# Position norms in groups of three chunks, zeroed states by copy, and new timetables

## The chip, the cores and the metric

The kernel runs on one core of a Trainium2 chip. The metric is the device time of one execution in microseconds, as the median of several runs. A profiled execution is one more run, recorded by the hardware profiler; its span is the time from the first to the last recorded instruction.

Five engines work side by side, each in the order of its own instructions: PE (matmuls; PEld are its weight loads), DVE (vector work), ACT (activation functions and copies), POOL (vector work of another kind) and SP, which here only issues DMA transfers.

## The reference, cut to what matters

The input x is 8 images of 256 channels and 48 x 48 positions (N = 2304). The parts that the change touches are these:

```
# layer 0, per image (after a group norm of x), with a residual
pos  = pos / max(norm(pos), 1e-12)
sim  = pos @ pos.T
topksim, topkid = top_k(sim, 16)
out  = sum(softmax(topksim) * feat[topkid])

# layer 1: two mamba layers in a row, with a group norm and a residual
dA = exp(dt_t[:, :, None] * A)
h  = h * dA + dt_t[:, :, None] * B_t[:, None, :] * x_t[:, :, None]
y  = einsum('bds,bs->bd', h, C_t)          # h starts as zeros
```

Each mamba layer has 512 inner channels and 16 states for each of them; A is minus the exponential of A_log. A layer also has a layer norm over the channels, an input projection, a convolution of four taps, a step size dt by softplus, a gate by silu and an output projection.

## The kernel before, in words

**Units.** The positions of an image are cut into six chunks of T = 384. A unit is one chunk c at one of the two mamba depths d. The 12 units of an image are run in the order (c,d) = (0,0), (1,0), (2,0), (0,1), (3,0), (1,1), (4,0), (2,1), (5,0), (3,1), (4,1), (5,1). The text calls these places positions 0 to 11 of an image. Positions 0 and 3 are the units with c = 0, in which the state begins as zeros.

**Steps and hooks.** A unit is 16 steps of 32 inner channels. The 128 partitions of a step are its 32 channels times four groups of states, with four states in each partition; a half takes two of these four. A half is a "hook": 32 hooks make a unit. Each hook has one scan on DVE (`run_scan`, L932, 128 x 770), whose factors are the decays that ACT makes by two exponentials (`decay`, L917) one hook ahead, in two PSUM banks. The scan's other input bx is made by POOL two steps ahead (`make_bx`, L893), and its first column is the state carried over from the chunk before. `take_up` (one step ahead) puts this in: an ACT copy out of `h_st` (L907), or for c = 0 a POOL memset (L905). After the scan the states are multiplied by C: on POOL for the halves with "G" in `SHARE` (`pool_part`, L960, issued a step later; two neighbouring halves in one instruction), on DVE for those with "V" (L934). `SHARE` has a row for each stage, see below. PE sums the states of four steps into y (`sum_states`, L975 and L978), the gate (L984) uses y, and ACT keeps the last column (`carry`, L948; `carry_pool`, L970).

**dt and dtx rows.** A step's rows come back from HBM in a replicated form by `load_rep` (L639), issued on SP: "dt" into one of three fixed buffers (step number modulo three), "dtx" into a pool of three.

**Timetables.** All else that a unit needs (input weights `load_in`, projections `in_proj`, taps, softplus, silu, gates, output projection) stands in two tables, `between` and `behind`, of entries (hook, function, arguments). A hook may be negative, since a unit's preparation lies in earlier units. At each hook the program issues, in this order:

```
        carry(m - 1)
        decay(m + 1)
        if p == 0:
            make_bx(n + LEAD)
            pool_part(n - 1)
            take_up(n + 1)
        else:
            carry_pool(n - 1)
```

then the `between` entries of that hook, the scan, the `behind` entries, and one piece of layer 0 of a later image (`ahead.go`). Nothing is reordered after that: the order of the program is each engine's order. There are three pairs of tables, one for each stage: beside the top-k of a later image (positions 1 to 9), `between_spare` and `behind_spare` (positions 10, 11 and 0), and the last image's own. An entry's stage goes by where its hook in the first pair lies.

**Layer 0 ahead.** `layer0` is a generator; each `yield` ends a hook's piece. Its projections and norms for image b run from hook 11 of position 11 of image b - 2 to about hook 28 of position 0 of image b - 1; its 18 blocks of similarities and top-k, 16 hooks each, then fill positions 1 to 9. Image 0's runs alone at the start. For a chunk, PE makes two projections (pp) and three features (pf), ACT copies them out (pos L363, feat L372) and squares pos, PE sums the norms (pn) and ACT takes them out into n2 (L377). The inverse root is Ln and Exp on ACT (`rsqrt_start`, L167 and L168) and one Newton step of five instructions on POOL (`rsqrt_end`, L175 to L179). `scale` spreads the result rn by PE (pb, L232) and multiplies pos by it on DVE (L324). All of this is done for each chunk, one chunk behind the projections.

Of the kernel before, what the change touches and what calls it, by code (L numbers as in the profile page):

```python
# [9 lines left out]
F32 = mybir.dt.float32  # L10
BF16 = mybir.dt.bfloat16
AF = mybir.ActivationFunctionType
# [4 lines left out]
P = 128  # L17
# [9 lines left out]
def tile_conv_preact(  # L27
# [46 lines left out]


    SHARE = (
        "GGVGGGVGGGVVGGVGGGGVGGGVGGGGGVVG",
        "GVGGGVVVGGVVGGGVVGGGVGVVGGVVGVGV",
        "VVVGVVGGGVVVGGVVGGGVGGVVVVGGGVVG",
    )  # L80
    assert N % T == 0 and N % P == 0 and T % P == 0 and NS % (J * HQ) == 0

# [145 lines left out]
    def spread(cols, n, psum, name):  # L228

        pb = psum(n * P, name)  # L230
        for j in range(n):
            nc.tensor.matmul(  # L232
                pb[:, j * P : (j + 1) * P], cols[:, j : j + 1].to_broadcast([P, P]), ident,
                start=True, stop=True,
            )
        return pb
# [24 lines left out]
    def layer0(b, left, pool, ps0, alone):  # L261
# [7 lines left out]
        def step(make, use):  # L269

            if len(pending) == depth:
                leave_psum()
            pending.append((make(), use))

        def leave_psum():
            if pending:
                made, use = pending.pop(0)
                use(made)
# [18 lines left out]
        pos = pool.tile([P, CB, N], F32, tag="pos", name=f"pos_{b}", bufs=1)  # L297
        feat = pool.tile([P, NB, C], F32, tag="feat", name=f"feat_{b}", bufs=1)
        n2, rn = {}, {}

        def normalized(c):
            xn = loaded.pop(c)
# [7 lines left out]
            return xn  # L310

        def inverse_norm(c):
            rn[c] = small.tile([P, TB], F32, tag="rn", name=f"rn_{b}_{c}")
            rsqrt_start(rn[c], n2[c], tiny[:, 1:2])

        def inverse_norm_end(c):
            rsqrt_end(nc.gpsimd, rn[c], n2[c], TINY, f"rn_{b}_{c}")

        def scale(c):


            def use(pb):
                cs = slice(c * T, (c + 1) * T)
                nc.vector.tensor_tensor(  # L324
                    pos[:, :, cs], pos[:, :, cs], pb.unsqueeze(1).to_broadcast([P, CB, T]), ALU.mult
                )

            step(lambda: spread(rn[c], TB, mm0, f"pb_{b}_{c}"), use)

        def chunk(c, xn):  # L330
            cs = slice(c * T, (c + 1) * T)
# [40 lines left out]
                return lambda pf: nc.scalar.copy(feat[:, c * TB + j, :], pf)  # L372

            def norm(pn):
                n2[c] = small.tile([P, TB], F32, tag="n2", name=f"n2_{b}_{c}")

                nc.scalar.activation(n2[c], pn, AF.Relu, bias=tiny[:, 0:1])  # L377

            for ob in range(CB):
                step(lambda: project(ob), position(ob))  # L380
# [12 lines left out]
        for c in range(NCH):  # L393
            yield from chunk(c, xn)
            if c + 1 < NCH:
                xn = normalized(c + 1)
            yield
            if c > 0:
                scale(c - 1)
                yield  # L400
        while pending:
            leave_psum()
# [3 lines left out]
        inverse_norm_end(NCH - 1)  # L406
        yield
        yield
        scale(NCH - 1)
        yield  # L410
        leave_psum()
        yield

        x1 = hbm.tile([C, N], F32, tag="x1", name=f"x1_{b}")
# [462 lines left out]
    def at(n):  # L877

        return units[n // STEPS], n % STEPS, n % STEPS // J
# [6 lines left out]
    def make_bx(n):  # L886


        if not 0 <= n < NSTEP:
            return  # L890
        unit, i, k = at(n)
        bx = keep.tile([P, Q, 1 + T], F32, tag="bx", name=f"bx_{n}", bufs=8)
        nc.gpsimd.tensor_tensor(  # L893
            bx[:, :, 1:], unit["BC"][0],
            unit["dtxr"][i].unsqueeze(1).to_broadcast([P, Q, T]), ALU.mult,
        )
        unit["bx"][i] = bx

    def take_up(n):

        if not 0 <= n < NSTEP:
            return
        unit, i, k = at(n)
        if unit["c"] == 0:
            nc.gpsimd.memset(unit["bx"][i][:, :, 0], 0.0)  # L905
        else:
            nc.scalar.copy(unit["bx"][i][:, :, 0], h_st[:, unit["d"], i])  # L907

    def decay(m):

# [90 lines left out]
    def leave(unit, cb):  # L1001
# [21 lines left out]
        (23, load_rep, "dt", 14), (5, load_rep, "dt", 5), (-4, load_bc, 1), (38, out_proj, 1), (17, load_d, 2),  # L1023
        (-17, tap, 1), (18, load_rep, "dtx", 13), (-8, times_x, 1), (21, gate, 1), (-22, normal),
        (1, load_rep, "dt", 3), (0, load_rep, "dtx", 4), (15, load_rep, "dt", 10), (6, load_rep, "dtx", 7),
        (10, load_rep, "dtx", 9), (11, gate, 0), (-29, spread_root), (-20, tap, 0), (-3, times_x, 3),
        (-19, load_in, 5), (33, load_out), (-3, load_rep, "dt", 0), (8, load_rep, "dtx", 8), (-22, load_in, 0),
        (21, load_rep, "dt", 13), (-10, step_size, 1), (9, copy_z, 2), (-18, in_proj, 2),
        (2, load_rep, "dtx", 5), (-21, load_in, 1), (10, sum_states, 0), (13, load_rep, "dt", 9), (9, silu_z),
        (7, load_rep, "dt", 6), (19, load_rep, "dt", 12), (-13, x_proj), (-6, load_rep, "dtx", 1),  # L1030
        (-14, load_in, 7), (-30, root), (9, load_rep, "dt", 7), (-24, load_in, 3), (17, load_rep, "dt", 11),
        (14, load_rep, "dtx", 11), (8, copy_z, 1), (-17, load_in, 6), (-3, load_d, 0), (4, load_rep, "dtx", 6),
        (-4, load_rep, "dtx", 2), (-42, load_v),
    ]
    behind = [
        (-12, split), (3, in_proj, 4), (-10, step_size, 0), (-8, load_rep, "dtx", 0), (-15, tap, 3),
        (-1, load_rep, "dt", 2), (-28, scale), (16, load_rep, "dtx", 12), (-35, square),
        (11, load_rep, "dt", 8), (8, in_proj, 6), (17, sum_states, 1), (-14, silu_x), (28, load_rep, "dt", 15),
        (-39, affine), (2, times_x, 2), (7, copy_z, 0), (19, load_rep, "dtx", 14), (10, load_rep, "dtx", 10),
        (-17, tap, 2), (-10, softplus), (-16, in_proj, 3), (36, gate, 3), (3, load_rep, "dt", 4),  # L1040
        (-3, load_rep, "dt", 1), (-29, load_in, 2), (5, in_proj, 7), (-15, taps, 1), (-2, load_rep, "dtx", 3),
        (38, leave, 1), (22, load_rep, "dtx", 15), (-8, load_in, 4), (29, load_d, 3), (-37, mean),
        (-19, taps, 0), (5, load_d, 1), (-19, in_proj, 1), (-10, load_bc, 0), (-30, root_end),
        (-9, times_x, 0), (29, gate, 2),
    ]
    between_spare = [
        (25, sum_states, 2), (-34, variance), (-21, in_proj, 0), (38, out_proj, 0), (-15, taps, 2),
        (-35, square), (39, leave, 0), (23, load_rep, "dt", 14), (5, load_rep, "dt", 5),
        (-1, load_rep, "dt", 2), (-4, load_bc, 1), (-7, times_x, 3), (38, out_proj, 1), (17, load_d, 2),
        (-17, tap, 1), (-8, times_x, 1), (19, gate, 1), (9, load_rep, "dtx", 8), (1, load_rep, "dt", 3),  # L1050
        (0, load_rep, "dtx", 4), (14, load_rep, "dt", 10), (6, load_rep, "dtx", 7), (11, load_rep, "dtx", 9),
        (-18, taps, 0), (12, load_rep, "dtx", 10), (17, load_rep, "dtx", 14), (11, gate, 0), (-1, times_x, 2),
        (-19, load_in, 5), (33, load_out), (3, load_rep, "dt", 4), (18, load_rep, "dtx", 13),
        (-22, load_in, 0), (29, load_d, 3), (21, load_rep, "dt", 13), (-20, tap, 0), (-10, step_size, 1),
        (-5, load_rep, "dt", 0), (9, copy_z, 2), (-18, in_proj, 2), (2, load_rep, "dtx", 5),
        (10, sum_states, 0), (13, load_rep, "dt", 9), (31, gate, 2), (9, silu_z), (7, load_rep, "dt", 6),
        (19, load_rep, "dt", 12), (-6, load_rep, "dtx", 1), (-14, load_in, 7), (37, gate, 3), (-31, root),
        (9, load_rep, "dt", 7), (5, load_d, 1), (-24, load_in, 3), (17, load_rep, "dt", 11),
        (14, load_rep, "dtx", 11), (-13, x_proj), (-17, load_in, 6), (-3, load_d, 0), (4, load_rep, "dtx", 6),
        (-4, load_rep, "dtx", 2), (-42, load_v), (-29, spread_root),  # L1060
    ]
    behind_spare = [
        (40, leave, 1), (-12, split), (-14, taps, 3), (-3, load_rep, "dt", 1), (4, in_proj, 4),
        (-10, step_size, 0), (-8, load_rep, "dtx", 0), (-15, tap, 3), (16, load_rep, "dtx", 12),
        (11, load_rep, "dt", 8), (8, in_proj, 6), (17, sum_states, 1), (-14, silu_x), (25, load_rep, "dt", 15),
        (-39, affine), (6, copy_z, 0), (-17, tap, 2), (-10, softplus), (-16, in_proj, 3), (7, in_proj, 5),
        (-27, load_in, 2), (6, in_proj, 7), (-15, taps, 1), (-2, load_rep, "dtx", 3), (8, copy_z, 1),
        (22, load_rep, "dtx", 15), (-16, load_in, 4), (-38, mean), (-22, normal), (-37, center),
        (-21, in_proj, 1), (-12, load_bc, 0), (33, sum_states, 3), (-30, root_end), (-9, times_x, 0),
        (-25, load_in, 1), (-28, scale),  # L1070
    ]
    between_last = [
# [135 lines left out]
```

## Time and profile before

| what | value |
|---|---|
| median of 3 runs | 9482.04 us (9474.05 to 9482.28) |
| profiled execution, its time | 9470.14 us |
| its span | 9468.4 us |
| granted TensorE clock in it | 0.899 |
| images 0 to 6, each (scan to scan) | about 1143 us |
| image 7 | 987.4 us |

The profile's busy times say how much an engine did, not what it waited for; the views of waits name, for each idle stretch, what ended it. A wait for several things is put down to the one that came last by the records. The table by windows gives the busy time of each engine in a stretch of the span, and so tells the stages apart.

### The profile page before, as it was taken

Reading aid. Unit: us, or ns where it says so; the run is one execution under the profiler, and the core shown is the slowest. Engines: PE = TensorE matmul, PEld = TensorE weight load, DVE = VectorE, ACT = ScalarE, POOL = GpSimd, SP = SyncE. Lnnn points to the kernel's source line nnn. Section 1 sums busy time; section 2 is a strip of 40 time slices with the busy share of each in tenths; the row PEclk is TensorE's granted clock in tenths of the full one; section 3 lists DMA queues with packets and bytes.
Section 4 is the critical chain, followed back from the end, with each engine's and each line's share of the span. In section 5 each row is a group of like instructions: output and inputs, shape, how many; then the busy total and the mean of one; then the engine's idle time right before and its main releaser. Section 6 shows DMA issues by size and latency. Waiting matters only on the chain.

```text
span 9468.4 us, 120581 instructions
## 1 busy us (share of the span) xinstructions
PE 7913.3 (84%) x37049; PEld 4429.9 (47%) x37049; DVE 8866.0 (94%) x7543; ACT 7297.1 (77%) x16042; POOL 8906.1 (94%) x3985
## 2 busy tenths in 40 slices
PE   8888987888878888788878888788887889877666
PEld 6744544454544554445444545444554445433332
DVE  6599998999989999899998999999999999989999
ACT  4578887778777877787878788778877888767776
POOL 2199999999999999999999999999999999999999
PEclk9989998899988998889988999889998999977887
DMA  4134444444444444444444434444444344444443
GB/s 127 47 126 135 133 136 148 130 136 137 136 147 131 130 141 132 149 128 139 130 143 137 138 128 138 140 141 131 139 133 154 126 139 130 137 154 145 149 146 125
DMA packets 1029829, 1275.92 MB, mean 135 GB/s; under 512 B 106528, under 2 KB 998944, under 8 KB 1028416
## 3 DMA queue, kind: packets, MB, share of 16 engines
q1 hardware_dynamic: 1028640, 1268.21, 41.4%
q8 instruction: 296, 4.85, 0.2%
q14 instruction: 349, 2.86, 0.1%
q10 hardware_dynamic: 544, 0.00, 0.0%
HBM read 1050.77 MB, written 217.06 MB: 134 GB/s over the span
## 4 chain that ended last, share of the span: by engine, by line
DVE 58%; ACT 12%; issue 11%; PE 11%; POOL 4%; DMA 2%; SPq 0%; DVEq 0%; POOLq 0%; ACTq 0%
DVE bx L932 21%; DVE da L932 13%; ACT da L917 5%; DVE xc L791 5%; DVE bx L934 4%; DVE top L470 4%; DVE top L465 3%; DVE left L472 3%; POOL bx L893 2%; DVE left L468 2%; PE pe L686 2%; PE y L978 2%; POOL bx L960 2%; PE pw L996 1%; DVE z L984 1%
## 5 line engine op out<-in xcount | busy, mean ns | idle before, releaser
L893 POOL TENSOR_TENSOR bx<-BC,dtxr 128x1536 f32<-128x1536 f32 x1536 | 5299.8, 3456 | 36.5 <-PE y L978 31.3
L917 ACT ACTIVATE da<-dtr,A_sb 128x385 f32<-128x385 f32 x6144 | 3592.7, 585 | 887.7 <-DVE bx L932 574.4
L932 DVE TENSOR_TENSOR_SCAN bx<-da,bx 128x770 f32<-128x770 f32 x1986 | 3417.5, 1745 | 129.0 <-ACT da L917 84.3
L960 POOL TENSOR_TENSOR bx<-bx,BC 128x1536 f32<-128x1536 f32 (+1 forms) x1317 | 3225.8, 2449 | 62.4 <-DVE bx L932 61.4
L932 DVE TENSOR_TENSOR_SCAN da<-da,bx 128x770 f32<-128x770 f32 x1086 | 1903.7, 1753 | 114.9 <-ACT da L917 108.6
L515 PE MATMUL po<-feat,aT 128*128 128x256 f32 x5184 | 1383.6, 416 | 229.0 <-ACT dt L830 93.2
L686 PE MATMUL pe<-vn,inw 128*128 128x384 f32 (+1 forms) x2976 | 1183.3, 526 | 202.7 <-ACT vn L763 86.0
L978 PE MATMUL y<-bx,sel 128*32 128x384 f32 x12288 | 1244.4, 531 | 94.6 <-POOL bx L960 90.2
L515 PEld LDWEIGHTS po<-feat,aT 128*128 128x128 f32 x5184 | 1027.4, 206 | 632.2 <-ACT aT L504 182.9
L444 PE MATMUL psim<-pos 128*128 128x512 f32 x2520 | 1182.3, 611 | 119.3 <-DVE xc L791 64.2
L934 DVE TENSOR_TENSOR bx<-da,BC 128x768 f32<-128x768 f32 x1086 | 1040.4, 958 | 37.4
L686 PEld LDWEIGHTS pe<-vn,inw 128*128 128x128 f32 x2976 | 562.1, 200 | 642.3 <-ACT vn L763 107.5
L978 PEld LDWEIGHTS y<-bx,sel 128*32 128x32 f32 x12288 | 398.0, 117 | 915.1 <-issue 701.0
L444 PEld LDWEIGHTS psim<-pos 128*128 128x128 f32 x2520 | 497.0, 207 | 694.0 <-issue 363.3
L791 DVE SCALAR_TENSOR_TENSOR xc<-pe,cw,xc 128x384 f32<-128x384 f32 x1080 | 653.9, 611 | 33.3 <-ACT xc L782 8.0
L504 ACT ACTIVATE aT<-pt 128x512 f32<-128x512 f32 (+1 forms) x720 | 387.5, 547 | 332.0 <-PE pt L496 329.8
L996 PE MATMUL pw<-z,ow 128*128 128x384 f32 x1536 | 549.2, 504 | 71.6 <-ACT aT L504 38.5
L495 PE MATMUL pt<-ident,sim 128*128 128x128 f32 x2592 | 537.0, 288 | 15.6 <-DVE v L750 7.2
L948 ACT COPY h_st<-da 128x2 f32<-128x2 f32 x884 | 139.5, 158 | 489.4 <-DVE bx L934 479.3
L975 PE MATMUL y<-xc,dmat 128*128 128x384 f32 x768 | 385.6, 588 | 153.2 <-ACT dt L830 37.6
L487 ACT ACTIVATE rest<-left,three 128x512 bf16<-128x512 f32 (+1 forms) x720 | 453.4, 669 | 63.7 <-DVE left L472 63.7
L496 PE MATMUL pt<-minus,rest 128*128 128x128 bf16 x2592 | 494.7, 224 | 2.8 <-ACT rest L487 2.8
(160 smaller groups left out, 9989.7 us busy)
## 6 DMA issues: line engine op xcount, KB each, us to landing
dtxr<-dtx_d SPq DMA_DIRECT2D x1536, 192.0 KB, 2.8
dtr<-dt_d SPq DMA_DIRECT2D x1536, 192.0 KB, 2.7
BC<-bc_d SPq DMA_DIRECT2D x192, 768.0 KB, 5.3
inw<-in_in_wT_dram SPq DMA_DIRECT2D x744, 128.0 KB, 2.5
dtx_d<-dtx SPq DMA_DIRECT2D x384, 192.0 KB, 1.9
dt_d<-dt SPq DMA_DIRECT2D x384, 192.0 KB, 2.0
ow<-in_out_wT_dram SPq DMA_DIRECT2D x96, 512.0 KB, 4.6
dmat<-diag SPq DMA_DIRECT2D x384, 64.0 KB, 2.5
```

Source lines behind the costliest of these rows:

```text
L444: nc.tensor.matmul(pm, pos[:, k, t * P : (t + 1) * P], pos[:, k, c0 : c0 + w], start=(k == 0), stop=(k == CB - 1),)
L495: nc.tensor.transpose(pt[:, q], row["sim"][:, r], ident)
L515: nc.tensor.matmul(row["po"], aT[:, m % PT, :], feat[:, m, :], start=(m == 0), stop=(m == NB - 1))
L686: nc.tensor.matmul(pe, w[:, k], unit["vn"][:, k, lo:], start=(k == 0), stop=(k == CB - 1))
L791: nc.vector.scalar_tensor_tensor(unit["xc"][e], unit["pe"][e][:, k : k + T], cw[:, unit["d"], e, k : k + 1], unit["xc"][e], ALU.mult, ALU.add,
L893: nc.gpsimd.tensor_tensor(bx[:, :, 1:], unit["BC"][0], unit["dtxr"][i].unsqueeze(1).to_broadcast([P, Q, T]), ALU.mult,)
L917: nc.scalar.activation(da[:, s * (1 + T) : (s + 1) * (1 + T)], unit["dtr"][i], AF.Exp, scale=A_sb[:, unit["d"], i, p * HQ + s : p * HQ + s ...
L932: nc.vector.tensor_tensor_scan(h, da, g, 0.0, ALU.mult, ALU.add)
L934: nc.vector.tensor_tensor(bx[:, :, 0:T], da.rearrange("p (q t) -> p q t", q=HQ)[:, :, 1:], unit["BC"][1][:, qs], ALU.mult,)
L960: nc.gpsimd.tensor_tensor(g[:, :, 0:T], g[:, :, 1:], unit["BC"][1][:, qs], ALU.mult)
L978: nc.tensor.matmul(y[j * G : (j + 1) * G, :], sel, unit["bx"][k * J + j][:, q, 0:T], start=False, stop=True, skip_group_check=True,)
L996: nc.tensor.matmul(pw, unit["ow"][:, k, cb * P : (cb + 1) * P], unit["z"][k], start=(k == 0), stop=(k == DB - 1),)
```

## The change

Four things are edited.

1. `take_up` copies from `h_st` on ACT also for c = 0. To this end `make_bx` zeroes the whole state of that depth (128 x 64) with one POOL memset, before it makes the first bx of such a unit.
2. In `layer0`, for all images but the first, the norms of three chunks (`many` = 3) share one tile n2 of nine columns, and Ln, Exp and the Newton step are done once for three chunks. `scale` comes three chunks behind the projections, and three of them at the end.
3. `SHARE` has new rows. The number of G and V halves in a unit of each stage stays as it was.
4. Entries of the two tables beside the top-k and of the two spare tables have other hooks, or stand in the other table of the pair.

```diff
     SHARE = (
-        "GGVGGGVGGGVVGGVGGGGVGGGVGGGGGVVG",
-        "GVGGGVVVGGVVGGGVVGGGVGVVGGVVGVGV",
-        "VVVGVVGGGVVVGGVVGGGVGGVVVVGGGVVG",
+        "GGVGGGVGGGVVGVGGGGGVGGGVGGGGGVVG",
+        "GVGGGVVVGGVVGGGGVGGVGGVVVGVVGVGV",
+        "VVGGVVGGGVVVGGVVGGGVGGVVGVGVGVVV",
     )
...
+        many = 1 if alone else NCH // 2
...
         def inverse_norm(c):
-            rn[c] = small.tile([P, TB], F32, tag="rn", name=f"rn_{b}_{c}")
-            rsqrt_start(rn[c], n2[c], tiny[:, 1:2])
+            if (c + 1) % many == 0:
+                g = c // many
+                rn[g] = small.tile([P, many * TB], F32, tag="rn", name=f"rn_{b}_{g}")
+                rsqrt_start(rn[g], n2[g], tiny[:, 1:2])
 
         def inverse_norm_end(c):
-            rsqrt_end(nc.gpsimd, rn[c], n2[c], TINY, f"rn_{b}_{c}")
+            if (c + 1) % many == 0:
+                g = c // many
+                rsqrt_end(nc.gpsimd, rn[g], n2[g], TINY, f"rn_{b}_{g}")
...
-            step(lambda: spread(rn[c], TB, mm0, f"pb_{b}_{c}"), use)
+            r = rn[c // many][:, c % many * TB : (c % many + 1) * TB]
+            step(lambda: spread(r, TB, mm0, f"pb_{b}_{c}"), use)
...
-            if c > 0:
-                scale(c - 1)
+            if c >= many:
+                scale(c - many)
                 yield
...
-        scale(NCH - 1)
-        yield
-        leave_psum()
+        for c in range(NCH - many, NCH):
+            scale(c)
+            yield
+        while pending:
+            leave_psum()
         yield
...
         unit, i, k = at(n)
+        if unit["c"] == 0 and i == 0:
+            nc.gpsimd.memset(h_st[:, unit["d"]], 0.0)
         bx = keep.tile([P, Q, 1 + T], F32, tag="bx", name=f"bx_{n}", bufs=8)
...
-        if unit["c"] == 0:
-            nc.gpsimd.memset(unit["bx"][i][:, :, 0], 0.0)
-        else:
-            nc.scalar.copy(unit["bx"][i][:, :, 0], h_st[:, unit["d"], i])
+        nc.scalar.copy(unit["bx"][i][:, :, 0], h_st[:, unit["d"], i])
```

Of the tables only the entries that differ are given here, as (hook, function, arguments):

| tables | before | after |
|---|---|---|
| beside the top-k | between: (-19, load_in, 5) | behind: (-27, load_in, 5) |
| | behind: (29, load_d, 3) | between: (31, load_d, 3) |
| | between: (-20, tap, 0) | behind: (-20, tap, 0) |
| spare | between: (19, load_rep, "dt", 12) | between: (17, load_rep, "dt", 12) |
| | behind: (33, sum_states, 3) | between: (35, sum_states, 3) |
| | behind: (6, in_proj, 7) | behind: (7, in_proj, 7) |
| | between: (4, load_rep, "dtx", 6) | behind: (4, load_rep, "dtx", 6) |

More of the change, by code (lines that the diff above doesn't have):

```diff
@@ L374, in norm @@
             def norm(pn):
-                n2[c] = small.tile([P, TB], F32, tag="n2", name=f"n2_{b}_{c}")
-                nc.scalar.activation(n2[c], pn, AF.Relu, bias=tiny[:, 0:1])
+                g, i = divmod(c, many)
+                if i == 0:
+                    n2[g] = small.tile([P, many * TB], F32, tag="n2", name=f"n2_{b}_{g}")
+                nc.scalar.activation(
+                    n2[g][:, i * TB : (i + 1) * TB], pn, AF.Relu, bias=tiny[:, 0:1]
+                )
             for ob in range(CB):
@@ L1025, in tile_conv_preact @@
         (1, load_rep, "dt", 3), (0, load_rep, "dtx", 4), (15, load_rep, "dt", 10), (6, load_rep, "dtx", 7),
[L1026 to L1033, printed above, removed]
+        (10, load_rep, "dtx", 9), (11, gate, 0), (-29, spread_root), (-3, times_x, 3), (33, load_out),
+        (-3, load_rep, "dt", 0), (8, load_rep, "dtx", 8), (-22, load_in, 0), (21, load_rep, "dt", 13),
+        (-10, step_size, 1), (9, copy_z, 2), (-18, in_proj, 2), (2, load_rep, "dtx", 5), (-21, load_in, 1),
+        (10, sum_states, 0), (31, load_d, 3), (13, load_rep, "dt", 9), (9, silu_z), (7, load_rep, "dt", 6),
+        (19, load_rep, "dt", 12), (-13, x_proj), (-6, load_rep, "dtx", 1), (-14, load_in, 7), (-30, root),
+        (9, load_rep, "dt", 7), (-24, load_in, 3), (17, load_rep, "dt", 11), (14, load_rep, "dtx", 11),
+        (8, copy_z, 1), (-17, load_in, 6), (-3, load_d, 0), (4, load_rep, "dtx", 6), (-4, load_rep, "dtx", 2),
+        (-42, load_v),
     ]
     behind = [
-        (-12, split), (3, in_proj, 4), (-10, step_size, 0), (-8, load_rep, "dtx", 0), (-15, tap, 3),
-        (-1, load_rep, "dt", 2), (-28, scale), (16, load_rep, "dtx", 12), (-35, square),
+        (-12, split), (3, in_proj, 4), (-10, step_size, 0), (-27, load_in, 5), (-8, load_rep, "dtx", 0),
+        (-15, tap, 3), (-1, load_rep, "dt", 2), (-28, scale), (16, load_rep, "dtx", 12), (-35, square),
         (11, load_rep, "dt", 8), (8, in_proj, 6), (17, sum_states, 1), (-14, silu_x), (28, load_rep, "dt", 15),
@@ L1040, in tile_conv_preact @@
         (-17, tap, 2), (-10, softplus), (-16, in_proj, 3), (36, gate, 3), (3, load_rep, "dt", 4),
-        (-3, load_rep, "dt", 1), (-29, load_in, 2), (5, in_proj, 7), (-15, taps, 1), (-2, load_rep, "dtx", 3),
-        (38, leave, 1), (22, load_rep, "dtx", 15), (-8, load_in, 4), (29, load_d, 3), (-37, mean),
+        (-3, load_rep, "dt", 1), (-29, load_in, 2), (5, in_proj, 7), (-20, tap, 0), (-15, taps, 1),
+        (-2, load_rep, "dtx", 3), (38, leave, 1), (22, load_rep, "dtx", 15), (-8, load_in, 4), (-37, mean),
         (-19, taps, 0), (5, load_d, 1), (-19, in_proj, 1), (-10, load_bc, 0), (-30, root_end),
@@ L1048, in tile_conv_preact @@
         (-35, square), (39, leave, 0), (23, load_rep, "dt", 14), (5, load_rep, "dt", 5),
[L1049 to L1057, printed above, removed]
@@ L1058, in tile_conv_preact @@
-        (9, load_rep, "dt", 7), (5, load_d, 1), (-24, load_in, 3), (17, load_rep, "dt", 11),
-        (14, load_rep, "dtx", 11), (-13, x_proj), (-17, load_in, 6), (-3, load_d, 0), (4, load_rep, "dtx", 6),
+        (-1, load_rep, "dt", 2), (-4, load_bc, 1), (35, sum_states, 3), (-7, times_x, 3), (38, out_proj, 1),
+        (17, load_d, 2), (-17, tap, 1), (-8, times_x, 1), (19, gate, 1), (9, load_rep, "dtx", 8),
+        (1, load_rep, "dt", 3), (0, load_rep, "dtx", 4), (14, load_rep, "dt", 10), (6, load_rep, "dtx", 7),
@@ new lines, in tile_conv_preact @@
+        (11, load_rep, "dtx", 9), (-18, taps, 0), (12, load_rep, "dtx", 10), (17, load_rep, "dtx", 14),
+        (11, gate, 0), (-1, times_x, 2), (-19, load_in, 5), (33, load_out), (3, load_rep, "dt", 4),
+        (18, load_rep, "dtx", 13), (-22, load_in, 0), (29, load_d, 3), (21, load_rep, "dt", 13), (-20, tap, 0),
+        (-10, step_size, 1), (-5, load_rep, "dt", 0), (9, copy_z, 2), (-18, in_proj, 2),
+        (2, load_rep, "dtx", 5), (10, sum_states, 0), (13, load_rep, "dt", 9), (31, gate, 2), (9, silu_z),
@@ L1060, in tile_conv_preact @@
+        (7, load_rep, "dt", 6), (17, load_rep, "dt", 12), (-6, load_rep, "dtx", 1), (-14, load_in, 7),
+        (37, gate, 3), (-31, root), (9, load_rep, "dt", 7), (5, load_d, 1), (-24, load_in, 3),
+        (17, load_rep, "dt", 11), (14, load_rep, "dtx", 11), (-13, x_proj), (-17, load_in, 6), (-3, load_d, 0),
         (-4, load_rep, "dtx", 2), (-42, load_v), (-29, spread_root),
@@ L1065, in tile_conv_preact @@
         (11, load_rep, "dt", 8), (8, in_proj, 6), (17, sum_states, 1), (-14, silu_x), (25, load_rep, "dt", 15),
[L1066 to L1069, printed above, removed]
+        (-39, affine), (4, load_rep, "dtx", 6), (6, copy_z, 0), (-17, tap, 2), (-10, softplus),
+        (-16, in_proj, 3), (7, in_proj, 5), (-27, load_in, 2), (7, in_proj, 7), (-15, taps, 1),
+        (-2, load_rep, "dtx", 3), (8, copy_z, 1), (22, load_rep, "dtx", 15), (-16, load_in, 4), (-38, mean),
+        (-22, normal), (-37, center), (-21, in_proj, 1), (-12, load_bc, 0), (-30, root_end), (-9, times_x, 0),
         (-25, load_in, 1), (-28, scale),
```

## The prediction

> **What bounds the kernel now.** The page comes first: busy time of each engine, then the chain that ended last.
>
> ```profile
> PE 7913.3 (84%) x37049; PEld 4429.9 (47%) x37049; DVE 8866.0 (94%) x7543; ACT 7297.1 (77%) x16042; POOL 8906.1 (94%) x3985
> ...
> DVE 58%; ACT 12%; issue 11%; PE 11%; POOL 4%; DMA 2%; SPq 0%; DVEq 0%; POOLq 0%; ACTq 0%
> ```
>
> DVE and POOL are equally full, but the chain is DVE's. These are averages, so the second view is a table by stage: of image 3 a unit beside the top-k (position 4) and positions 10 and 11, position 0 of image 4, and a stretch of image 7.
>
> ```profile
> 4283.00:4379.90 96.90, 85.40 (x412) 48.55 (x411) 95.44 (x83) 78.44 (x177) 95.14 (x36) 0.95 0.44 141
> 4856.80:4947.60 90.80, 64.01 (x307) 33.45 (x306) 82.10 (x76) 67.16 (x154) 86.97 (x43) 0.82 0.44 145
> 4947.60:5043.20 95.60, 75.46 (x320) 40.16 (x316) 81.20 (x71) 73.62 (x148) 88.96 (x46) 0.82 0.47 154
> 5043.20:5138.80 95.60, 77.39 (x357) 42.95 (x358) 84.67 (x76) 74.21 (x161) 90.36 (x67) 0.87 0.45 143
> 8900.00:9000.00 100.00, 68.92 (x299) 33.06 (x298) 92.89 (x77) 77.41 (x176) 99.18 (x37) 0.83 0.43 142
> ```
>
> The columns are the length, then the busy time of PE, PEld, DVE, ACT and POOL. Beside the top-k (positions 1 to 9) DVE idles 1.5 us in 96.9: it is the bound, and only a wait of DVE itself can be gained there. In positions 10, 11 and 0 DVE idles 8.7, 14.4 and 10.9 us, 34 us an image: no engine is full, single waits set the time. Image 7 has POOL at 99%. The third view says which waits, DVE's in the window of positions 10, 11 and 0 (times in us: total, count, longest):
>
> ```profile
> DVE bx L932 <- ACT da L917: 10.4, 5, 4.4
> DVE da L932 <- ACT da L917: 6.3, 6, 2.5
> DVE z L984 <- PE y L978: 6.1, 3, 2.5
> DVE bx L932 <- POOL dtx L841: 2.5, 1, 2.5
> DVE v L750 <- PE lb L232: 2.2, 1, 2.2
> DVE pos L324 <- PE pb L232: 1.7, 1, 1.7
> ...
> DVE bx L932 <- POOL bx L905: 0.5, 1, 0.5
> ```
>
> Most are scans that wait for decays (L917), which stand behind bursts of other ACT work; POOL stands only behind the pos wait (pb waits for rn, L179), the memset row, and by name the dtx row, whose scan also waits for decays. A change that mostly lightens POOL can therefore take only a part of the 34 us.
>
> **Zeroed states.** 256 memsets (L905) leave POOL, 16 memsets of a whole state take their place, ACT gets 256 more copies. All DVE waits for L905 in the whole trace make 22.9 + 1.5 = 24.4 us. The timeline at position 3 of image 3 shows why:
>
> ```profile
> 4193.76 3.20 POOL L960 TENSOR_TENSOR bx<-bx,BC 128x1536 f32<-128x1536 f32 x1
> 4196.87 0.13 POOL L905 MEMSET bx<- 128x4 f32 x1
> ...
> 4193.51 1.74 DVE L932 TENSOR_TENSOR_SCAN bx<-da,bx 128x770 f32<-128x770 f32 x1
> 4197.03 1.76 DVE L932 TENSOR_TENSOR_SCAN bx<-da,bx 128x770 f32<-128x770 f32 x1 [1.78 <-POOL bx L905]
> ```
>
> The memset stands behind the 3.20 us multiply of the step before, which cannot start before that step's scan; its own 0.13 us is not the cost. An ACT copy has no such predecessor: its product (L893) was ready 4 to 15 us ahead, and its state was zeroed long before. The row for such copies is 181 ns, and ACT idles 18 us in such a unit. Of the 24.4 us, 6.6 are the very first scan, which goes on waiting for the first product: a loss of about 0.2 us there. What is left is 17.8: about 1.77 in position 3 of images 0 to 5 and 2.8 in image 6, 0.55 in position 0, 1.6 at the start. The 16 copies of a unit at 0.18 add 2.9 us to ACT; where DVE waits for ACT (position 0) some of it may show. I take **-16**. The bounds are -17.8 and, if all copies of position 0 fall into ACT's bursts (7 images x 2.9 = 20), +2.
>
> **Newton steps.** Per image six groups of five POOL instructions become two, six pairs of Ln and Exp become two. The row of L175 is 196 ns, L178 228, the other three 193 to 194: 1.01 us a group, 1.4 us from first start to last end, and up to 3.9 with waits for ACT's rn. Four groups less are 5.6 to 9 us of POOL per image and 4 x (0.290 + 0.204) = 2.0 us of ACT. POOL idles 5 to 7 us in positions 11 and 0, so this is not gained as such; only the waits named after it are. The scaling of pos by chunk (L324) follows its rn by three chunks, not one, so the projections of layer 0 come up to three hooks sooner on PE and ACT, and the multiplies later. The pos wait of 1.74 us at hook 27 of position 11 goes (its multiply is no longer there): 6 x 1.7 = **-10**. At hook 4 of position 0 a scan waits 1.42 us for decays behind ACT's copy of a projection that stands on PE behind y3, which is blocked by POOL's last multiply; with the projections ahead of y3 on PE this goes: 6 x 1.4 = **-8.5**. Position 11 waits 2.50 and 4.36 us at hooks 20 and 24, position 0 waits 1.88 and 1.32 at hooks 12 and 20, behind ACT bursts; with less ACT work near them I take 2 of these 10.1 us: 6 x 2 = **-12**, between 0 and -60. What is late next: the moved multiplies may wait for PE's pb in position 0, like the one that goes; I take 1 us an image, **+6**, between 0 and 6 x 1.7 x 3 = 31. The last multiply stays at hook 28, so the next image's similarities do not start later.
>
> **SHARE.** The counts of POOL and DVE halves in a unit stay as they are in all three rows; one to three multiplies (DVE 958 ns; POOL 1690 for a half, 3185 for both) change places. Beside the top-k POOL trails DVE by 0.1 to 7 us there and y1 has 1.3 to 3.5 us to spare: nothing. In image 7 32 memsets at 0.06 us from start to start give **-2**; the new row of that image can cost or bring as much as one half multiply in each of 12 units, 12 x 0.96 = 12 us; I take nothing.
>
> **Timetables.** Two entries matter. First, in positions 10, 11 and 0 the load of step 12's dt goes from hook 19 to hook 17. Its buffer is that of step 9, so it now waits on SP for the first decay pair of step 9, and the second pair (which then reads step 12's row) waits on ACT for the load. Behind it on SP stands step 11's dt, on ACT the silu burst. The trace of before has no such stall, but it has its parts: in position 10 of image 3 the pairs lie at 4905.0 to 4906.2 and 4908.3 to 4909.5, 2.1 us apart; dt loads land after 2.7 us (median), 2.4 at the least. So ACT is late by 0.4 to 0.8 us, and the scan of hook 19 starts 4.4 us after its decays: hidden there. Behind it the burst waits 1.2 to 1.3 us for DVE's taps, which hides most again. I take 0.3 x 21 units = **+6**, between 0 and the worst wait of ACT for a dt load in the trace, 2.3 x 21 = 48.
>
> A rule against this edit: the Trainium skill, "DMA: Bandwidth & Descriptors", Rules for kernel authors, says to issue a load early, compute, and wait late, so that its fixed cost overlaps; here nothing overlaps. Its fit (Anatomy of one DMA: about 2.0 us plus bytes at 436 GB/s, measured on another issuing path) makes, as an estimate, 2.45 us for these 192 KB, which would put ACT about 0.35 us late and the term at about 0, for a sum of 6 us less.
>
> Second, beside the top-k input weights 5 are loaded earlier, and take the buffer that in-projection 7 leaves; input weights 1 then wait on SP for in-projection 0. Between these two projections lie 3.0 to 3.8 us on PE, filled by other matmuls, and the load lands after
>
> ```profile
> DMA to landing us min/median/max: 2.1/2.5/4.8
> ```
>
> so in-projection 1 starts as before in the median; DVE needs its product much later. SP's next dt load is about 1.7 us late with 12 us to spare. I take 0 here. The other moved entries change no engine's order before a consumer that is due, or have ten and more us in front of it: 0.
>
> **Sum** on the profiled execution (9470.1): -16 - 10 - 8.5 - 12 + 6 - 2 + 6 = -36.5, so 9433.6. That execution is 11.9 us under the median of the runs (9482.0), so I forecast 9445.5, -0.4%. A measurement of this kernel tells about 0.2%, 19 us, from no change.
>
> **Rivals.**
> *Slower: in-projection 1 is held up beside the top-k.* Place: SP stands at input weights 1, PE at in-projection 1, in 9 units of 7 images, 63. Behind it on PE stand the similarity matmuls, behind these ACT's copies, and DVE's top (L465, whose waits for them are already 52.6 us). For it: DVE has no slack there. Against: the median landing fits, and PE idles 9 to 11 us a unit. With landing at 4.8 us PE is 1.4 us late; passed on in full 63 x 1.4 = 88, net +52: 9534. It decides from 0.9 us a unit (63 x 0.9 = 57, net +20).
> *Only the memsets.* The waits in positions 10, 11 and 0 are bursts of ACT, and a wait that goes reappears at the next burst. Then -16 and -2 are left, less the dt stall: 9464 to 9470, within the bound. For it: 17 of the 30 us listed are decays by name.
> *POOL was what held the bursts.* If the 9 us less on POOL free y3 and with it PE and ACT, half of positions 11's and 0's 25 us go: 6 x 12.5 = 75, with the memsets' 16: 9391. For it: PE waits 90 us for L960; against: few of these waits are followed by one of DVE.
> *The Newton grouping does not do what it says:* the later rn makes the first pos multiplies wait, 18 to 31 us given back: 9464 to 9477.
>
> **How the numbers follow.** Forecast 0.53, larger gain 0.15, only memsets or given back 0.15, slower 0.17. Range: low end by the larger gain, 9395; high end takes in the middle rivals and the lesser cases of the slower one, 9502. Faster 0.70, same 0.13, slower 0.17.
>
> **What would show it.** In the profile after: no DVE wait for L905; position 3 of images 0 to 5 shorter by 1.8 us, positions 1, 2 and 4 to 9 unchanged; no pos wait in position 11; ACT waiting 0.4 to 0.8 us for a dt load in 21 units without a DVE wait behind it; position 11 shorter by 3 us, 0 by 2 to 3. Wrong, if units beside the top-k grow, if PE waits for the inw load before in-projection 1, or if DVE's waits for decays grow by what the others lose.

## The result, and the profile after

The changed kernel takes 9423.9 us (median; 9422.3 to 9431.3) against 9479.2 us before in the same comparison: a ratio of 0.9947, 95% interval 0.9932 to 0.9961. That is 55 us faster by the medians and 50, 0.5%, by the ratio. The profiled execution takes 9422.8 us, 47.3 us less than the one of before, with a granted clock of 0.898 against 0.899.

The page of the profile after, the busy times and the first line of the chain:

```profile
PE 7867.0 (84%) x37049; PEld 4423.6 (47%) x37049; DVE 8867.3 (94%) x7543; ACT 7307.1 (78%) x16242; POOL 8867.9 (94%) x3605
...
POOL 1%; issue 0%; PE 0%; DVE 0%; DMA 0%; POOLq 0%; ACT 0%; SPq 0%
```

POOL is busy for 38 us less and has 380 instructions less, ACT for 10 us more; DVE's work is the same to 1.3 us, so DVE gained only waiting time. The chain broke off in this trace after 1% of the span, and nothing is read from it.

The table by windows, for the same units as in the prediction (position 4, 10 and 11 of image 3, position 0 of image 4, a stretch of image 7; length, then busy PE, PEld, DVE, ACT, POOL):

```profile
4255.10:4352.00 96.90, 83.77 (x409) 47.22 (x408) 95.44 (x81) 78.56 (x177) 95.03 (x36) 0.95 0.43 139
4829.00:4918.60 89.60, 62.86 (x308) 32.55 (x308) 82.08 (x76) 67.09 (x154) 88.95 (x44) 0.82 0.46 149
4918.60:5010.00 91.40, 71.85 (x317) 39.34 (x315) 80.18 (x71) 72.66 (x146) 88.99 (x36) 0.84 0.52 167
5010.00:5105.30 95.30, 75.52 (x359) 42.78 (x358) 85.61 (x77) 74.51 (x171) 87.29 (x43) 0.86 0.42 135
8873.00:8973.00 100.00, 75.83 (x318) 36.09 (x316) 94.87 (x82) 74.43 (x166) 98.07 (x35) 0.81 0.45 143
```

Position 4 is as long as before (96.9). Position 10 is 1.2 us shorter, position 11 4.2, position 0 0.3. In position 10 POOL now works 88.95 of 89.6 us.

The same count over the whole trace, from the first scan of a unit to that of the next, after minus before, summed over images 0 to 6: position 11 -31.9, position 3 -12.3, position 10 -8.3, position 2 -3.5, position 0 +5.4, all others together +5.1; image 7 +0.5, the start -1.7. Positions 0, 2 and 3 trade up to 2.5 us an image with each other from trace to trace (the timetables alone, which change no time that can be told, show +11.3, -8.8 and +4.7 there), so only their sum is read, and position 3 only beside its own wait. Position 11 takes part: it is 6.6 us shorter with the timetables alone and 10.3 with the zeroed states alone. Its sum, too, is read beside the waits in it.

DVE's waits in positions 10, 11 and 0 after the change:

```profile
DVE da L943 <- ACT da L928: 15.8, 9, 4.2
DVE bx L943 <- ACT da L928: 4.7, 6, 1.5
DVE z L995 <- PE y L989: 3.9, 2, 2.5
DVE lv L183 <- ACT nt_rs L182: 0.7, 1, 0.7
DVE v L732 <- PE lm L726: 0.5, 1, 0.5
```

In these three units the waits for lb (the layer norm's inverse root, spread by PE), pb and the memset are gone; over seven images position 11's wait for lb falls from 18.0 us to 6.3. Scans waiting for decays (the first two rows) still make 20.5 us, against 16.7 before, or 19.2 with the scan that stood under the dtx row. So these waits as a whole have not shrunk; the one at hook 20 has, as the experiments show. The rest is small.

### The profile page after: what moved, and what is told of

Read it like the earlier page. It is cut to its first block, busy times and chain, and to the rows that moved or that the text cites. A ratio compares the mean times of both kernels' runs of the same rounds, so it can differ in the third digit from the quotient of the medians.

```text
span 9421.1 us, 120485 instructions
## 1 busy us (share of the span) xinstructions
PE 7867.0 (84%) x37049; PEld 4423.6 (47%) x37049; DVE 8867.3 (94%) x7543; ACT 7307.1 (78%) x16242; POOL 8867.9 (94%) x3605
## 5 line engine op out<-in xcount | busy, mean ns | idle before, releaser
L456 PE MATMUL psim<-pos 128*128 128x512 f32 x2520 | 1203.2, 619 | 130.6 <-DVE xr L551 85.4
L989 PE MATMUL y<-bx,sel 128*32 128x384 f32 x12288 | 1221.6, 527 | 72.7 <-POOL bx L971 72.4
L507 PE MATMUL pt<-ident,sim 128*128 128x128 f32 x2592 | 540.1, 289 | 13.4 <-DVE v L762 5.6
```

The costliest lines, as they stand in the source:

```text
L456: nc.tensor.matmul(pm, pos[:, k, t * P : (t + 1) * P], pos[:, k, c0 : c0 + w], start=(k == 0), stop=(k == CB - 1),)
L507: nc.tensor.transpose(pt[:, q], row["sim"][:, r], ident)
L989: nc.tensor.matmul(y[j * G : (j + 1) * G, :], sel, unit["bx"][k * J + j][:, q, 0:T], start=False, stop=True, skip_group_check=True,)
```

## The experiments

Ratios and intervals are each kernel's against the kernel before in the same comparison (9473 to 9475 us there). Each part was first put alone on the kernel before. Idle times "at a hook" are those of DVE between the scan before that hook's and the hook's own, added up from the trace over images 0 to 6.

**Zeroed states alone.**

```diff
+        if unit["c"] == 0 and i == 0:
+            nc.gpsimd.memset(h_st[:, unit["d"]], 0.0)
...
-        if unit["c"] == 0:
-            nc.gpsimd.memset(unit["bx"][i][:, :, 0], 0.0)
-        else:
-            nc.scalar.copy(unit["bx"][i][:, :, 0], h_st[:, unit["d"], i])
+        nc.scalar.copy(unit["bx"][i][:, :, 0], h_st[:, unit["d"], i])
```

> The kernel before with the zeroed states alone (one POOL memset of the state, ACT copies in place of the small memsets). Theory (order on POOL: the memset stood behind the multiply of the step before): DVE's waits for the memset go, 1.2 to 1.8 us in position 3 of images 0 to 5 and 2.7 in image 6, 0.5 in position 0, together -14 to -18 us; all other units as before within 0.3 us. Rival (the memsets' own work on POOL): only image 7, where POOL is full, gains, 32 x 0.06 = -2 us, and position 3 stays at 95.8 us. Second rival (the copies load ACT): position 0 grows by up to 2.9 us, and the sum comes to about 0.

Measured: 9451.5 us, ratio 0.9979 (0.9969 to 0.9988), about -20 us (-29 to -11). No DVE wait for the memset is left, position 3 is shorter by 10.8 us over seven images (0.9 to 1.9 each), image 7 by nothing. The order on POOL was the cost, not the memset's own 0.1 us: the rival that asked for a gain in image 7 alone is out, and so is the second one's sum of 0. Position 0 is 8.5 us longer over seven images, as that rival said, but it is 11.3 longer with the timetables alone, which have no such copies, so this is no sign of them.

**Grouped norms alone** (`many` and the lines of `layer0` in the diff).

> The kernel before with the position norms of three chunks at once alone. Theory (the scaling that comes three chunks later takes two waits out of position 11, the one for lb at hook 5 and the one for pb at hook 27): position 11 of images 0 to 5 shorter by 3.5 to 4.5 us; position 0 gains its wait at hook 4 (1.4) and loses it again to new waits at hooks 3, 10 and 13, net 0 to +2; together -15 to -27 us. Rival (the position 11 gain comes from SHARE or the tables): position 11 shorter by under 1.5 us, in all under -10 us. The prediction on record had -10 and -8.5 from the two named waits and -12 +6 around them, -24.5.

Measured: 9468.3 us, 0.9995 (0.9986 to 1.0005), which is no change that can be told. Position 11 is 15.9 us shorter over seven images, position 0 12.1 longer. DVE's waits in position 11 of image 3 and then in position 0 of image 4 of this kernel:

```profile
DVE bx L944 <- ACT da L929: 4.1, 2, 3.9
DVE da L944 <- ACT da L929: 3.8, 3, 2.5
DVE v L762 <- PE lb L232: 2.0, 1, 2.0
DVE z L996 <- PE y L990: 1.2, 1, 1.2
...
DVE bx L944 <- ACT h_st L982: 3.0, 2, 2.0
DVE z L996 <- PE y L990: 2.0, 1, 2.0
DVE bx L944 <- ACT da L929: 1.5, 2, 1.0
DVE da L944 <- ACT da L929: 1.4, 2, 0.9
DVE da L944 <- ACT h_st L982: 1.3, 1, 1.3
DVE da L944 <- POOL bx L917: 0.7, 1, 0.7
DVE lv L183 <- ACT nt_rs L182: 0.6, 1, 0.6
```

The pb wait left position 11, as expected (idle time at hook 27 from 8.3 us to 0.2). But it leaves with the zeroed states alone as well (0.2), and in all images but one with the timetables alone (1.9), so its going can't be put down to the grouping alone. The wait for lb stays at 2.0 us in this image. In position 0 the idle time at hooks 4 and 12 falls from 22.7 to 8.7 us, and at hooks 3, 10, 11 and 13 it rises from 16.9 to 42.2: there ACT now has the copies and squares of layer 0, which come sooner (at hook 3 also the grouped Ln and Exp), in front of what DVE waits for. Hooks 3, 10, 12 and 13 look like this in all five kernels with the grouping, and in none without it. So what the part takes away it puts back one unit later.

**SHARE alone** (the three rows of the diff).

> The kernel before with the new SHARE rows alone. Theory formed from the trace of the changed kernel (a DVE multiply moved from behind the decays of hook 20 to ahead of them fills the wait of that hook): positions 10, 11 and 0 each shorter by 0.9 to 1.3 us in images 0 to 6, together -18 to -26 us; beside the top-k and in image 7 no change within 0.3 us a unit. Rival (the prediction on record): nothing, 0 within 3 us. Second rival (half of it): only position 10 gains, 7 x 1.2 = -8 us.

Measured: 9434.8 us, 0.9959 (0.9944 to 0.9973), -40 us: the largest part, and twice the theory. Position 10 is 8.4 us shorter over seven images, position 11 26.2, position 0 1.8; beside the top-k (positions 4 to 9) and in image 7 nothing beyond 1.7 us over seven images.

**Timetables alone** (the entries of the change; the second half of step 9 in positions 10, 11 and 0 reads step 12's dt row).

> The kernel before with the new timetables alone; as in the changed kernel, the second half of step 9 in positions 10, 11 and 0 reads the dt row of step 12. Theory of the record: ACT waits 0.4 to 0.8 us for the dt load in 21 units and most of it is hidden, +6 us (0 to +48); beside the top-k nothing. Rival: the tables give part of the gain (position 10 or 11 shorter by 1 us and more), -8 us or better. Second rival: in-projection 1 is late beside the top-k, +0.3 us or more in each of 63 units, +20 us.

Measured: 9473.2 us, 1.0000 (0.9990 to 1.0009). Nothing, within 9 us either way.

The four parts alone make -23 - 7 - 40 - 2 = -72 us in medians, the whole -55 (-50 by its ratio on this base). Next, which row of SHARE it is, and how the parts add up.

**The second row of SHARE alone.**

```diff
-        "GVGGGVVVGGVVGGGVVGGGVGVVGGVVGVGV",
+        "GVGGGVVVGGVVGGGGVGGVGGVVVGVVGVGV",
```

> The kernel before with the second row of SHARE alone (positions 10, 11 and 0): the DVE multiplies behind the scans of hooks 15 and 20 go to hooks 19 and 24. Theory (a multiply of 0.96 us that stands directly in front of a scan that waits for an ACT burst costs nothing, and the wait at hook 27 of position 11 goes with it): the whole gain of all three rows, -34 to -40 us, position 10 shorter by 1.2 us, position 11 by 3 to 6. Rival (the rows beside the top-k and of image 7 bring part of it): under -25 us.

Measured: 9427.5 us, 0.9952 (0.9937 to 0.9966), -46 us. All of SHARE's gain is in this row, four letters of 32, which hold in 21 units.

**The changed kernel with the old SHARE.**

> The changed kernel with the SHARE rows of before. Theory A (the parts are independent, SHARE is worth 40): slower than the changed kernel by 35 to 40 us, that is -12 to -20 us against before. Theory B (the parts remove the same waits of position 11 and gains overlap by some 20 us): slower than the changed kernel by 15 to 25 us, that is -30 to -40 us against before.

Measured: 9464.6 us, 0.9990 (0.9981 to 1.0000). It lies 41 us above the changed kernel's 9423.9 (medians of two comparisons). Theory A holds: SHARE is worth its 40 us in company too. The other three parts together bring 9 us, less than the zeroed states alone; that the norms and tables take back what the copies gave is likely, but the two intervals overlap, and it is not shown. In its trace DVE idles 12.3 us at hooks 28 and 29 of position 11 and 11.8 at hook 10 of position 0, where before it idles 0.2 and nothing.

**Zeroed states and SHARE, without norms and tables.**

> The kernel before with the zeroed states and the new SHARE rows, without the grouped norms and the new tables. Theory A (independent): -60 us against before, faster than the changed kernel by 5 to 10 us. Theory B (overlap in position 11): -45 to -55 us, the same as the changed kernel within 8 us; the norms and tables are then worth nothing on top.

Measured: 9416.7 us, 0.9942 (0.9927 to 0.9957), -57 us. It lies between the two theories, and cannot be told from the changed kernel (0.9947). Norms and tables add nothing that can be told on top of these two.

**The changed kernel with the old timetables.**

> The changed kernel with the timetables of before. Theory (the record: the dt load of step 12 costs 0 to 0.3 us in each of 21 units, the rest nothing): faster than the changed kernel by 0 to 8 us. Rival (the tables were fitted to the other parts and bring what these lack): slower than the changed kernel by 10 us and more, with position 0 growing.

Measured: 9416.6 us, 0.9944 (0.9927 to 0.9960). Also the same within the intervals; a fit of the tables to the other parts is ruled out as a large term.

**One pair of the second row: hook 15 to POOL, hook 19 to DVE.**

```diff
-        "GVGGGVVVGGVVGGGVVGGGVGVVGGVVGVGV",
+        "GVGGGVVVGGVVGGGGVGGVVGVVGGVVGVGV",
```

> The kernel before with one pair of the second SHARE row alone: the half of hook 15 goes from DVE to POOL, that of hook 19 from POOL to DVE. Theory D (DVE: its multiply of 0.96 us stands in front of the scan of hook 20, which waits for ACT, and costs nothing there): the wait at hook 20 shrinks by 0.96 us or goes, in positions 10, 11 and 0 of images 0 to 6, 21 x 1.0 = -20 us, and the waits at hooks 26 and 27 of position 11 stay. Theory P (POOL: it no longer runs out of work at steps 8 to 10, is less behind later, and so the waits for lb and pb in position 11 shrink): -25 us and more, position 11 shorter by over 2.5 us. Rival: 0, both pairs are needed.

Measured: 9442.7 us, 0.9966 (0.9953 to 0.9979), -31 us. DVE's timeline around hook 20 of position 11, first of before, then of this kernel (start, duration, instruction, idle before it):

```profile
5000.49 1.90 DVE L791 SCALAR_TENSOR_TENSOR xc<-pe,cw,xc 128x384 f32<-128x384 f32 x3
5002.30 0.55 DVE L984 TENSOR_TENSOR z<-y,z 128x384 f32<-128x384 f32 x1
5002.77 1.75 DVE L932 TENSOR_TENSOR_SCAN bx<-da,bx 128x770 f32<-128x770 f32 x1
5007.02 1.77 DVE L932 TENSOR_TENSOR_SCAN da<-da,bx 128x770 f32<-128x770 f32 x1 [2.50 <-ACT da L917]
```

```profile
4986.42 1.90 DVE L791 SCALAR_TENSOR_TENSOR xc<-pe,cw,xc 128x384 f32<-128x384 f32 x3
4988.23 0.55 DVE L984 TENSOR_TENSOR z<-y,z 128x384 f32<-128x384 f32 x1
4988.69 1.76 DVE L932 TENSOR_TENSOR_SCAN da<-da,bx 128x770 f32<-128x770 f32 x1
4990.49 0.96 DVE L934 TENSOR_TENSOR bx<-da,BC 128x768 f32<-128x768 f32 x1
4992.95 1.77 DVE L932 TENSOR_TENSOR_SCAN da<-da,bx 128x770 f32<-128x770 f32 x1 [1.50 <-POOL bx L960]
```

The multiply (L934) moved into the 2.50 us in which DVE stood, and 1.50 are left. (The row's releaser is the last one by the records; a POOL multiply ended just there.) Why DVE stood there shows ACT's timeline of before: the decays of hook 19, then the silu burst with its two table loads, and only after it the decays of hook 20 (those of the last row; rows for layer 0 in between).

```profile
4997.12 1.20 ACT L917 ACTIVATE da<-dtr,A_sb 128x385 f32<-128x385 f32 x2 [1.44 <-DVE bx L932]
4998.26 0.18 ACT L907 COPY bx<-h_st 128x4 f32<-128x4 f32 x1
4998.45 1.28 ACT L797 ACT_TABLE_LOAD   x1
4999.74 1.35 ACT L799 ACTIVATE xc<-xc 128x384 f32<-128x384 f32 x3
5002.42 0.52 ACT L799 ACTIVATE xc<-xc 128x384 f32<-128x384 f32 x1 [1.33 <-DVE xc L791]
5002.96 1.28 ACT L800 ACT_TABLE_LOAD   x1
...
5005.73 1.19 ACT L917 ACTIVATE da<-dtr,A_sb 128x385 f32<-128x385 f32 x2
```

What the burst waits for last is DVE: its fourth silu (L799 at 5002.42, 1.33 us idle) stands until the taps of the convolution (L791) that began at 5000.49 end at 5002.39, and these stand on DVE between the scans of hooks 18 and 19. From there to the decays of hook 20 ACT does not wait again. So DVE work ahead of these taps delays the end of the burst, and work behind them lies inside it. The half of hook 15 stood ahead of them, that of hook 19 stands behind them. In before the fourth silu waits for the taps in 20 of the 21 units, 1.2 to 1.3 us. How the burst begins counts for less: the decays of hook 19 wait for the scan of hook 17 in this unit (1.44 us) and for nothing in position 0, and the gain is nearly the same.

This is theory D. The idle time at hook 20 falls from 7.3 to 0.6 us in position 10, from 16.8 to 9.3 in position 11 and from 9.2 to 2.5 in position 0, together by 20.9 us, where 21 x 1.0 was expected; hooks 26 and 27 of position 11 keep their waits (12.2 us of 12.3), as it said. In the six kernels without this pair hook 20 makes 33 to 35 us in these units, in the eight with it 12 to 16.

Position 11 gains 14.4 over seven images, more than theory D's 7. The rest is at hook 5, where the wait for lb falls from 18.0 to 9.5 us, and there POOL's side shows. In before, POOL ran out of work inside the burst, and stood idle for the scan of hook 19:

```profile
4998.01 1.68 POOL L960 TENSOR_TENSOR bx<-bx,BC 128x768 f32<-128x768 f32 x1
4999.65 3.44 POOL L893 TENSOR_TENSOR bx<-BC,dtxr 128x1536 f32<-128x1536 f32 x1
5004.66 3.17 POOL L960 TENSOR_TENSOR bx<-bx,BC 128x1536 f32<-128x1536 f32 x1 [1.57 <-DVE bx L932]
```

With a half more of work it does not, and at the end of position 10 of image 4 its last multiply ends 5.4 us after the last scan, not 6.4. On this multiply stands PE's y3 (the unit's last sum of states), behind it lb, behind it DVE's v at hook 5 of position 11: that wait falls from 2.2 us (position 11 of image 3) to 1.2. The wait for lb also differs among kernels without the pair (13.9 to 18.0 us over seven images), so not all of the 8.5 us need be the pair's; with the pair it is under 10 in all eight. Both theories hold, D with the larger share.

**The other pair: hook 20 to POOL, hook 24 to DVE.**

```diff
-        "GVGGGVVVGGVVGGGVVGGGVGVVGGVVGVGV",
+        "GVGGGVVVGGVVGGGVVGGGGGVVVGVVGVGV",
```

> The kernel before with the other pair of the second SHARE row alone: the half of hook 20 goes from DVE to POOL, that of hook 24 from POOL to DVE. Theory D (a multiply behind the wait of hook 24 fills no wait, one taken away behind hook 20's wait shortens nothing): -5 to +3 us. Theory P (a half fewer for POOL right behind the burst of hook 24, where it is late): the waits at hooks 26 and 27 of position 11 (0.67 and 1.5 to 1.7) go and lb comes sooner, 6 x 3 = -15 to -25 us.

Measured: 9463.1 us, 0.9989 (0.9979 to 0.9998), -10 us. DVE's waits in position 11 of image 3:

```profile
DVE da L932 <- ACT da L917: 6.4, 2, 4.4
DVE bx L932 <- ACT da L917: 2.9, 2, 2.5
DVE pos L324 <- PE pb L232: 2.7, 1, 2.7
DVE v L750 <- PE lb L232: 2.2, 1, 2.2
```

The interval, -20 to -2 us, reaches into both theories' ranges, so the time does not decide between them. In the trace theory P is met in part: the wait at hook 26 of position 11 is gone (4.0 us over seven images, now 0), but the pb wait at hook 27 is not. In this image it grew from 1.7 to 2.7 us, while image 4's went; over seven images it is 8.0 us, as before (8.1), and the wait for lb is 17.4, against 18.0. Over seven images position 11 is 5.4 us shorter and position 0 4.2 longer, no more than these two trade. The two pairs make -31 - 10 = -41, the row -46: they add up within the intervals. Only with the whole row are both waits gone, hooks 26 and 27 idling 0.2 us in place of 12.3.

**The dt load of step 12 back at hook 19, in the changed kernel.**

```diff
-        (7, load_rep, "dt", 6), (17, load_rep, "dt", 12), (-6, load_rep, "dtx", 1), (-14, load_in, 7),
+        (7, load_rep, "dt", 6), (19, load_rep, "dt", 12), (-6, load_rep, "dtx", 1), (-14, load_in, 7),
```

> The changed kernel with the load of step 12's dt back at hook 19 in positions 10, 11 and 0. Theory from the two traces (ACT's waits of 2.0 us for this load at hook 19 only take the place of waits of 1.4 us for DVE and 0.7 us for the taps): the same as the changed kernel within 4 us, the 21 waits for the load gone. The prediction on record: faster by 6 us (0 to 48). Rival (the later load helps something else on SP): slower by 5 us and more.

Measured: 9424.0 us, 0.9945 (0.9928 to 0.9961), against 0.9947 with the load at hook 17. No difference can be told, but the intervals are wider than the 6 us in question; the traces say more. In the changed kernel ACT does wait there, in all 21 units; its timeline in position 10 of image 3:

```profile
4876.17 1.21 ACT L928 ACTIVATE da<-dtr,A_sb 128x385 f32<-128x385 f32 x2
...
4880.17 1.20 ACT L928 ACTIVATE da<-dtr,A_sb 128x385 f32<-128x385 f32 x2 [2.06 <-DMA dtr<-dt_d]
...
4884.77 0.52 ACT L811 ACTIVATE xc<-xc 128x384 f32<-128x384 f32 x1 [0.63 <-DVE xc L803]
```

The pairs are now 4880.17 - 4877.38 = 2.8 us apart, 0.7 more than before, and the wait for the taps behind them is 0.63 us, not 1.32. The 0.7 us is taken out of that wait, and the burst ends when it did: position 10 is 89.63 us long with either load. In positions 11 and 0 of images 0 to 6 the cover is used up. With the load at hook 17 the fourth silu waits there for the taps 0.1 us or not at all, and DVE idles 15.5 us at hook 20; with the load at hook 19 it waits 1.3 us (all but one unit), and DVE idles 11.8. So the load does show, with 3.7 us.

**A version from these findings: one more half, from hook 16 to hook 9**, on the kernel with the zeroed states and SHARE.

```diff
-        "GVGGGVVVGGVVGGGGVGGVGGVVVGVVGVGV",
+        "GVGGGVVVGVVVGGGGGGGVGGVVVGVVGVGV",
```

> The kernel before with the zeroed states and the new SHARE rows (as in the earlier run of these two), and one more pair of the second row: the half of hook 16 goes from DVE to POOL, that of hook 9 from POOL to DVE, directly behind the start of the silu burst of hook 9. Theory D (a multiply of 0.96 us behind the start of a burst and ahead of the scans that wait for it is free): the waits at hooks 10 and 11 shrink by 0.96 us in each of 21 units, -20 us against that run, so -70 to -80 us against before. Theory P (what counts is how far POOL is behind, and POOL gets a half later): the same as that run within 6 us, -52 to -62 us. Rival (the gate at hook 11 waits for y and not for DVE, so the multiply only takes the place of that wait's beginning in positions 10 and 0, and the half that leaves hook 16 lets the silu burst of hook 18 start sooner): -8 to -14 us against that run.

Measured: 9407.7 us, 0.9930 (0.9916 to 0.9943), -66 us against before, and 9 below the run without this pair (9416.7). That is the rival's figure, but theory P's can't be told from it: the intervals overlap, and the profiled executions of the two lie 0.6 us apart (9407.7 and 9408.3). DVE's waits in position 10 of image 3, without and with the pair:

```profile
DVE z L983 <- PE y L977: 2.5, 1, 2.5
DVE da L931 <- POOL dtx L841: 2.3, 1, 2.3
DVE da L931 <- ACT da L916: 1.5, 2, 1.1
DVE bx L931 <- ACT da L916: 0.2, 1, 0.2
```

```profile
DVE da L931 <- ACT da L916: 2.9, 2, 2.3
DVE z L983 <- PE y L977: 2.5, 1, 2.5
```

The wait of 1.1 us at hook 10 is gone (6.5 us of waits became 5.4), and position 10 is 1.0 us shorter in every image, position 11 1.5 on the average, position 0 nothing: there (image 5) POOL ends its last multiply 5.4 us after the last scan, against 2.9 without the pair. Where theory D looked, it was right: the idle time at hook 10 of position 10 and at hook 11 of positions 11 and 0 falls from 36.7 to 16.2 us, 21 x 0.98. But other hooks take it back: position 2 is 10.6 us longer over seven images, and in position 0 hooks 1 and 4 idle 5.9 us more. So the rival's reason, that the multiply only fills the beginning of a wait in positions 10 and 0, is not what the trace shows, and its figure is luck. This kernel's median is the lowest of all; its interval and the changed kernel's meet between 0.9932 and 0.9943, so against the changed kernel the 0.2% is likely, not certain.

## Why the prediction was right or wrong

The direction and the range were right, and the sum (-36.5 on the profiled executions, -47.3 measured; forecast 9445.5, measured 9423.9) came out near, but by luck: two errors offset each other. The steps that failed are SHARE, put at nothing and worth 40 us, and the +6 for what the Newton grouping makes late, which was about 25. Term by term:

**Zeroed states, -16: right.** Position 3 gives -12.3 in the whole change, where the waits made 13.4, and alone the part gives -20 (-29 to -11). The mechanism was the one stated: a short instruction behind a long one on an engine in order. No cost of the copies to DVE is seen.

**Newton steps, -10 - 8.5 - 12 + 6 = -24.5: mis-sized, and this step failed as a sum.** Alone it brings -7 by the medians (-13 to +5). At the places that the step named, the idle time falls by 25 us with this part alone, where it said 30.5: hook 27 of position 11 by 8.1, hook 24 there by 3.0, hooks 4 and 12 of position 0 by 3.9 and 10.1. (Hook 27 loses its wait with other parts alone too, and hook 4 with the timetables alone, so some of this is not the grouping's.) The warning that something would be late next was right, but its price of +6 was too low: hooks 3, 10, 11 and 13 of position 0 gain 25.3 us of idle time. It was not the moved multiplies that were late, as the step and the last rival had it: they wait for pb 0.1 us in the whole changed kernel after its first image, and not at all with this part alone. DVE waits for ACT there, behind layer 0's copies and squares, which come sooner. The last rival had the size, 18 to 31 us, with another cause.

**SHARE, "nothing": wrong, and the largest term of all.** The step counted the halves and found the counts equal, looked at what the moves do beside the top-k, and left it there. In positions 10, 11 and 0 they take a DVE multiply from ahead of the taps for which the silu burst waits to behind them. Alone the part is -40 us, and its second row -46. The prediction itself names two of the three waits that this shortens, at hook 20 of position 11 (2.50 us) and of position 0 (1.32); the third, in position 10, is 1.04 us, and a multiply is 0.96. 21 x 1.0 would have been the term, and POOL's part comes on top. In position 10, to which the prediction gave no term, each image is 1.2 us shorter.

**The dt load, +6: about 4 by the traces.** In position 10 ACT's pair came 0.7 us late, inside the 0.4 to 0.8 forecast, and the cover that was named, the wait for the taps, hides all of it. The wait in the profile, 2.0 us, is no measure of the delay there, since 1.4 of it was a wait for DVE before. In positions 11 and 0 the delay takes the whole cover of 1.3 us, and 3.7 us show at hook 20 over seven images. The measured times can't tell this from 0 or from 6. The estimate of 2.45 us from the Trainium skill ("DMA: Bandwidth & Descriptors", Anatomy of one DMA) was too short for this queue: 2.8 us lie between the pairs, and the dt rows land after 2.8 in the median of this trace.

**In-projection 1, 0: right.** PE waits for these weights in 7 of the 63 units, 2.2 to 2.4 us at hook 13 of position 1, and none of positions 4 to 9 is longer by more than 1.5 us over seven images; position 1 is as long as before. The prediction named such a wait of PE as a sign of being wrong; it came in these 7 units and cost nothing that shows. The slower rival did not come.

**Image 7, -2: nothing** (+0.5 in the profile).

**The rivals.** "Only the memsets" is what the change would have been without SHARE: -9 us, within the bound. So the 0.70 for faster rested on a sum whose second term brings little or nothing, and the forecast was saved by a term that had been put at nothing. Position 0, which was to be 2 to 3 us shorter, is 0.8 us longer an image.

What stays open: why the zeroed states bring 20 us alone but the three parts without SHARE only 9, and why positions 0, 2, 3 and 11 trade time with each other.

## What to carry to other kernels

When work moves between engines or places at equal counts, don't put it down as nothing: look for the bursts of another engine that the bound engine waits for, find the last thing of the bound engine that each burst waits for, which need not be what it begins with, and ask of each moved piece whether it lies ahead of that point or behind it. A piece of 0.96 us moved from ahead of it to behind it took 1.0 us of waiting out of each of 21 units. The rows of SHARE brought 40 us, the other three edits without them 9. A wait that is taken away from a unit with several other waits is worth little until the next unit has been looked at as well.

## What the runs showed of the hardware

A wait for a load can look three times as long as the delay that it makes: in position 10 a wait of 2.06 us stood for 0.7 us of delay, and the unit takes the same 89.63 us with and without it. The Newton step on nine columns takes about the time of that on three: 204 ns for the last multiply against 194.

```profile
L179 POOL TENSOR_TENSOR rn<-rn,nt_rn 128x9 f32<-128x9 f32 x14 | 2.9, 204 | 1.2
...
L179 POOL TENSOR_TENSOR rn<-rn,nt_rn 128x3 f32<-128x3 f32 x6 | 1.2, 194 | 0.5
```
